# Turning the masks of a graph network by DMA instead of on TensorE, eleven in each of two stages

## The chip, the core and the metric

One of the eight cores of a Trainium2 chip runs the whole program. The metric is device microseconds of one execution. The engines are called as the profile calls them: PE is TensorE (PEld its weight loads), DVE is VectorE, ACT is ScalarE, POOL is GpSimd and SP is SyncE, which only issues DMAs here.

## What is computed

A graph of 2708 nodes has 512 features a node (x, float32) and a dense symmetric adjacency matrix adj (int32, about 2.3% ones, with a full diagonal). Four layers follow each other, each as `x = layernorm(x + layer(x, adj))`. What matters for the change is layer 0:

```
Ab   = adj > 0
keep = Ab & (cumsum(Ab, axis=1) <= 64)        # the first 64 neighbours of a row
cnt  = keep.sum(axis=1)
nb   = (keep @ x) / max(cnt, 1)
x0   = leaky(x @ W_line.T + b_line) + where(cnt > 0, leaky(nb @ W_nb.T + b_nb), 0)
```

Layer 1 uses all neighbours (`mask @ x / deg`) and a pair of dense products; layers 2 and 3 are graph attention over the same mask, layer 3 with a feed-forward net behind it. So every layer reads one mask, and layer 0 reads besides which ones are among the first 64 of their row.

## The kernel before, in words

The rows are cut into 22 tiles of 128 (the last has 20). The mask is needed transposed, since a matmul contracts over partitions. It lies in one tile that stays to the end, `maskT`, 128 partitions x 22 tiles x 2816 columns in fp8: element (p, j, c) belongs to neighbour 128 j + p of node c. Its sign tells two things: -1 is a neighbour among the first 64, +1 a later one, 0 none. Layer 0 takes `Relu(-maskT)` (line 369, into `kT`), later layers take it as it is different from zero (line 525).

A mask, that is the 128 rows of one row tile, is made in these steps:

- `load_mask` (line 272): a DMA on POOL's queue reads 128 x 2708 int32 and casts to bf16, into a buffer `m`.
- `count` (line 277): one activation on ACT over the whole width; its accumulator gives the row's degree, `cnts`.
- `place` (lines 283 and 286): on DVE a scan along the row counts up from -64.5 and stops at 0.5 (`OP.min` with a half), and a product with the mask leaves a negative number on the first 64 ones, a positive one on the rest and 0 elsewhere. In stage 1 a row is done in two parts, in stage 2 in four, each part a scan and a product.
- `turn` (lines 288 to 304): 22 PE transposes of 128 x 128 (line 295) against a bf16 identity, in three groups of up to eight, each group into one PSUM bank; after each group ACT takes the sign from PSUM into `maskT` (line 299). Last, a small DMA on POOL's queue copies the 20 rows of the last row tile to partitions 32 to 51 (line 302).

The program runs in stages. Only the first two are touched.

**Stage 1** (line 307 on) walks the 22 row tiles. Per tile it transposes x on PE (line 133), copies it to SBUF on ACT (line 135, `xT`), multiplies it by W_nb (line 259; the result is split into `yH` on ACT, line 231, and `yL` on DVE, line 236) and by W_line (line 259 again, into the single buffer `pm1`), whose result gets its bias and its leaky relu on DVE (lines 352 and 195) and goes to DRAM through POOL's queue (line 354). The order of PE is written out by hand here: `pe(...)` ties each PE instruction behind the one before. Among these steps the first `HERE` masks are made: one per tile in most tiles, with the turn of a mask a tile after its count. `issue_after` ties the count behind `yH` and the two parts of the scan behind `yL` and behind the relu. Mask buffers `m` are three. x is fetched on SP's queue into three buffers (line 173).

**Stage 2** (line 360 on) is the sum `keep @ x W`. The row tiles are taken in blocks, first the two last (20 and 21), then five blocks of four (`cuts`), and the masks are made in that same order (`turns`). A block runs over the 22 column tiles j: ACT makes `kT` for the next j (line 369, two buffers), and PE adds `kT.T @ yH` and `kT.T @ yL` into one PSUM bank per row tile (line 496). A block needs its masks complete. At each j two generators are advanced by a step: `todo`, which finishes the row tiles of the block before (lines 414 to 421, DVE mainly, with `r0` and x fetched on SP's queue), and `both`, which runs the remaining masks (`other_masks`), then the weights of layer 1 (`weights1`), then small vectors of layers 2 and 3 (`vectors`). `both` stands behind the `kT` of the next j (`issue_after`). Each `yield` ends a step. A mask of `other_masks` takes eleven steps before the change: one for the count and one empty, four for the parts of the scan, two empty ones, three for the groups of the turn. Its buffers are two rooms, `w` (the place of a weight) and `spare`.

Behind stage 2 follow layer 1 (a second stage of products, in which DVE takes the signs out of `maskT`, then sums over the mask, line 547) and the two attention layers with the feed-forward net. Between the engines the order of instructions is set by a scheduler that keeps the program's dependencies and the `issue_after` ties; each engine then runs its own list in order, and waits on semaphores.

Of the kernel before, what the change touches and what calls it, by code (L numbers as in the profile page):

```python
# [11 lines left out]
BF16 = mybir.dt.bfloat16  # L12
F8 = mybir.dt.float8e4
AF = mybir.ActivationFunctionType
# [4 lines left out]
P = 128  # L19
# [7 lines left out]
STEP = 2.0 ** 68  # L27
# [3 lines left out]
def kernel(  # L31
# [9 lines left out]
    nc = tc.nc  # L41
    N = x.shape[0]
    NT = -(-N // P)
    FULL = N // P
# [5 lines left out]
    def rows(t):  # L50
        return min(P, N - t * P)
# [11 lines left out]
    identb = const.tile([P, P], BF16, name="identb")  # L63
    nc.vector.tensor_copy(identb, ident)
    G = 8
# [16 lines left out]
    maskT = big.tile([P, NT, NT * P], F8, name="maskT")  # L82
# [12 lines left out]
    few = N - (NT - 1) * P  # L95
    LAST, TWIN = NT - 1, 32
# [61 lines left out]
    def early(first, n, make):  # L158

        made = {}  # L160

        def get(i, **how):
            for j in range(len(made), min(i + first + 1, n)):
                made[j] = make(j, **how)
            return made[i]
        return get
# [36 lines left out]
    with ExitStack() as phase:  # L203
        yp = phase.enter_context(tc.tile_pool(name="y", bufs=1))
        cnts = yp.tile([P, NT], F32, name="cnts")
# [56 lines left out]

        HERE = NT - 8
        cuts = [(b, min(b + 4, NT)) for b in range(0, NT, 4)]
        cuts = cuts[-1:] + cuts[:-1]
        turns = [t for b in cuts for t in range(*b)]

        def load_mask(i, m):  # L270
            n = rows(turns[i])
            nc.gpsimd.dma_start(m[:n], adj[turns[i] * P:turns[i] * P + n, :], max_dma_last_dim=N * 2)
            return m

        def count(i, m):
            t, n = turns[i], rows(turns[i])
            nc.scalar.activation(m[:n], m[:n], AF.Sigmoid, bias=gate[:n], scale=STEP, accum_out=cnts[:n, t:t + 1])

        def place(i, m, places, part, of):

# [4 lines left out]
                                         OP.add, OP.min)  # L285
            return nc.vector.tensor_mul(m[:n, c0:c1], m[:n, c0:c1], places[:n, :c1 - c0])

        def turn(i, m, psum, order=as_it_comes):
            t, n = turns[i], rows(turns[i])
            for g0 in range(0, NT, G):  # L290
                g1 = min(g0 + G, NT)
                ps = psum()
                for j in range(g0, g1):
                    w = rows(j)
                    order(nc.tensor.transpose(ps[:w, j - g0, :n], m[:n, j * P:j * P + w], identb[:n, :n]))
                parts = [(P, g0, min(g1, FULL))] + ([(rows(FULL), FULL, NT)] if g1 > FULL else [])
                for w, a, b in parts:
                    if a < b:
                        nc.scalar.activation(maskT[:w, a:b, t * P:t * P + n], ps[:w, a - g0:b - g0, :n], AF.Sign,
                                             saturate=False)  # L300
                if g1 == NT:
                    nc.gpsimd.dma_start(maskT[TWIN:TWIN + few, LAST, t * P:t * P + n],
                                        maskT[:few, LAST, t * P:t * P + n])
                yield

        def rows_of(src):
            return early(2, NT, lambda t: fetched(src, t, rows(t)))

        with ExitStack() as ph:
            st = ph.enter_context(tc.tile_pool(name="l0a", bufs=1))  # L310
            wnT, wlT = weight(), weight2
            room = [maskT[:, G + k, :4 * D].bitcast(F32) for k in range(2 * KD)]

            xs = rows_of(x)
            xTs = early(0, NT, lambda t, order=as_it_comes: transposed(ahead, ps_tr, xs(t), rows(t), "xT", order))

            transpose_weight(room[:KD], ps_tr, wnT, l0_w_nb, (nc.sync, nc.scalar))
            lows = {}  # L320
            for t in range(2):
                xT = xTs(t, order=pe)
                lows[t] = keep_y(t, P, product(xT, P, wnT, 0, pe))
            transpose_weight(room[KD:], ps_tr, wlT, l0_w_line)
            b_line = bias(bcast(l0_b_line, D))
            masks = early(1, HERE, lambda i: load_mask(i, st.tile([P, N], BF16, name="m", bufs=3)))
            masks(0)
            nc.gpsimd.memset(maskT[:, NT - 1, :], 0.0)
            nc.gpsimd.memset(maskT[:, :, N:], 0.0)
            counted = turned = 0  # L330
            for t in range(NT):
                n = rows(t)
                if t > 1:

                    lows[t] = keep_y(t, n, product(xTs(t, order=pe), n, wnT, 0, pe, sums() if t % 2 else None))
                xT = xTs(t)
                if t + 1 < NT:
                    xTs(t + 1, order=pe)
                while turned < counted - (t + 2 < NT):
                    for _ in turn(turned, masks(turned), lambda: sums(BF16, (P, G, P)), pe):  # L340
                        pass
                    turned += 1
                now = counted < min(HERE, -(-(t - 1) * HERE // (NT - 5)))
                if now:
                    m, places = masks(counted), st.tile([P, N // 2], BF16, name="places", bufs=1)
                    with tc.issue_after(highs[t].ins):
                        count(counted, m)
                    with tc.issue_after(lows[t].ins):
                        place(counted, m, places, 0, 2)
                pm = product(xT, n, wlT, 1, pe)  # L350
                u = sm.tile([P, D], F32, name="u")
                nc.vector.tensor_add(u[:n], pm[:n], b_line[:n])  # L352
                low = rows_made = leaky(u[:n], u[:n])
                nc.gpsimd.dma_start(r0_dram[t * P:t * P + n, :], u[:n])
                if now:
                    with tc.issue_after(low.ins):
                        place(counted, m, places, 1, 2)
                    counted += 1
# [3 lines left out]
        with ExitStack() as ph:  # L362
# [9 lines left out]
            def other_masks():  # L372

                def room(i):
                    r = (ahead.tile([P, 2 * KD * (D + 2 * H)], BF16, name="w", tag="w", bufs=1) if i % 2 else
                         st.tile([P, 2 * KD * D], BF16, name="spare", tag="spare"))
                    m = r[:, :N]
                    load_mask(i, m)
                    return m, r[:, N:N + N // 4 + 1]

                got = {HERE: room(HERE)}
                for i in range(HERE, NT):
                    if i + 1 < NT:
                        got[i + 1] = room(i + 1)
                    m, places = got.pop(i)
                    if i == HERE:
                        for _ in range(5):
                            yield
                    count(i, m)
                    yield  # L390
                    yield
                    for part in range(4):
                        place(i, m, places, part, 4)
                        yield
                    yield
                    yield
                    psum = (ps_mm.tile([P, G, P], BF16, name=f"pm{k % 2}") for k in range(3))
                    for _ in turn(i, m, lambda: next(psum)):
                        yield
                nc.vector.tensor_scalar(iso, cnts, 0.5, None, op0=OP.is_lt)  # L400
                nc.vector.tensor_scalar(rdeg, cnts, 1.0, None, op0=OP.max)
                nc.vector.reciprocal(rdeg, rdeg)
# [83 lines left out]
            for i, b in enumerate(cuts):  # L486
                ts_ = range(*b)
                pa = {t: sums() for t in ts_}
                for j in range(NT):
                    if j + 1 < NT:  # L490
                        nxt, nxt_made = kept(b, j + 1)
                    elif i + 1 < len(cuts):
                        nxt, nxt_made = kept(cuts[i + 1], 0)
                    for t in ts_:
                        for y in halves(j):
                            nc.tensor.matmul(pa[t], kT[:, (t - b[0]) * P:(t - b[0] + 1) * P], y[:, j, :],  # L496
                                             start=(j == 0 and y is yH), stop=(j == LAST))
                    kT = nxt
                    if j % 3:
                        next(todo, None)  # L500
                    with tc.issue_after(nxt_made.ins):
                        next(both, None)
                with tc.issue_after(nxt_made.ins):
                    reciprocals(slice(*b))
                us = {}
                for t in ts_:
                    n = rows(t)
                    us[t] = st.tile([P, D], F32, name=f"u{t - b[0]}")
                    nc.scalar.activation(us[t][:n], pa[t][:n], AF.Copy, scale=rkeep[:n, t:t + 1])
                todo = finish(ts_, us)  # L510
# [6 lines left out]
            for t in range(NT):  # L517
                n = rows(t)
# [989 lines left out]
```

## Time and profile before

| what | value |
|---|---|
| time, median of 3 runs | 2926.25 us (2925.69 to 2927.17) |
| the profiled execution: time | 2926.44 us |
| its span, first to last instruction | 2924.5 us |
| mean granted TensorE clock | 0.996 |
| PE / DVE / ACT / POOL busy | 2842.8 / 1983.5 / 1499.8 / 244.8 us |
| first and last PE transpose of a mask, stage 1 | 50.1 and 195.2 us |
| the same, stage 2 | 221.2 and 376.1 us |
| first sum (line 496) | 202.54 us |

A line of the order of time gives start, duration, engine, line, operation, output and inputs, shapes and how many instructions are merged; in brackets stands the idle time of the engine before it, and who ended it. In the table of DMA issues the last number is the median time from issue to landing. In the table of queues stand packets, megabytes and the time of their packets as a share of 16 DMA engines over the span. PE's matmuls are pipelined, so the time of a run of matmuls is read from start to start.

### The profile page before, as it was taken

The numbers are of one execution on the slowest core, as the hardware profiler recorded it, in microseconds if no ns is written. First come the engines' busy times: TensorE is split into PE (matmuls) and PEld (weight loads), VectorE is DVE, ScalarE is ACT, GpSimd is POOL, SyncE is SP. The second block draws the span as 40 slices with busy tenths as digits, with TensorE's granted clock in tenths as the row PEclk, the third lists the DMA queues.
The fourth block names the chain that finished last, engine by engine and source line by source line (L and its number), as shares of the span: only waits on it lengthen the run. The fifth ranks groups of instructions, "written<-read, shape, count | busy, mean of one in ns | idle before, by whom it ended". The sixth has DMA issues, their size and how long they took to land. (4 is left out here: it accounts for less than half of the span.)

```text
span 2924.5 us, 36470 instructions
## 1 busy us (share of the span) xinstructions
PE 2842.8 (97%) x14370; PEld 1584.3 (54%) x14370; DVE 1983.5 (68%) x2341; ACT 1499.8 (51%) x1749; POOL 244.8 (8%) x387
## 2 busy tenths in 40 slices
PE   8999999999999999999999999999999999999997
PEld 4557766458888333444466443444375555555555
DVE  6866637542334999999978999999954435435342
ACT  3546532112322999999965999999951000000001
POOL 1111101101110000000012000000200010100000
PEclk9999999999999999999999999999999999999999
DMA  5633426322222111111143111110161000000000
GB/s 130 131 88 72 109 80 184 123 63 91 83 72 78 33 37 36 35 45 39 38 142 122 37 37 36 45 51 34 35 160 60 4 26 15 26 15 16 15 22 21
DMA packets 122518, 181.58 MB, mean 62 GB/s; under 512 B 43007, under 2 KB 67908, under 8 KB 122338
## 3 DMA queue, kind: packets, MB, share of 16 engines
q1 hardware_dynamic: 92470, 117.50, 13.5%
q0 software_dynamic: 18864, 57.45, 6.9%
q10 hardware_dynamic: 11004, 4.22, 0.6%
q8 instruction: 115, 1.88, 0.3%
q14 instruction: 65, 0.53, 0.1%
HBM read 148.91 MB, written 44.65 MB: 66 GB/s over the span
## 5 line engine op out<-in xcount | busy, mean ns | idle before, releaser
L752 DVE SCALAR_TENSOR_TENSOR e<-v_bc,ucol,maskT 128x1408 f32<-128x1408 f32 (+3 forms) x804 | 1133.7, 1477 | 322.3 <-PE pn L1135 312.8
L781 ACT ACTIVATE c<-e,bcol 128x1300 fp8e4<-128x1300 f32 (+2 forms) x688 | 956.6, 1412 | 63.4 <-DVE e L752 18.6
L953 PE MATMUL po<-e,R 128*64 128x512 f32 (+3 forms) x4224 | 894.7, 548 | 26.3 <-DVE e L752 24.3
L953 PEld LDWEIGHTS po<-e,R 128*64 128x64 f32 (+1 forms) x4224 | 333.4, 136 | 554.7 <-issue 390.4
L1135 PE MATMUL pn<-e,R 128*128 128x512 f32 (+3 forms) x1056 | 403.0, 545 | 1.1 <-DVE lin L1155 0.3
L1135 PEld LDWEIGHTS pn<-e,R 128*128 128x128 f32 (+1 forms) x1056 | 183.9, 190 | 197.1 <-issue 181.5
L1085 ACT ACTIVATE w<-pl,b 128x256 f32<-128x256 f32 (+1 forms) x88 | 40.9, 465 | 371.0 <-PE pl L1083 371.0
L496 PE MATMUL acc<-yH,kT 128*128 128x512 f32 x484 | 195.2, 409 | 4.7 <-ACT kT L369 4.5
L547 PE MATMUL acc<-yH,mf 128*128 128x512 f32 x484 | 185.0, 389 | 0.0
L496 PE MATMUL acc<-yL,kT 128*128 128x512 f32 x462 | 180.8, 391 | 0.0
L547 PE MATMUL acc<-yL,mf 128*128 128x512 f32 x462 | 179.7, 389 | 0.0
L122 POOL TENSOR_TENSOR ln_rs<-ln_rs,half 128x1 f32<-128x1 f32 (+1 forms) x88 | 53.0, 602 | 1397.7 <-DVE ln_rs L121 1348.4
L674 PE MATMUL pm<-w,xT 128*128 128x264 f32 (+1 forms) x704 | 165.1, 387 | 3.4 <-ACT xT L135 1.6
L259 PE MATMUL pm<-weight,xT 128*128 128x512 f32 (+1 forms) x344 | 158.4, 604 | 8.2 <-DVE u L352 6.8
L1083 PE MATMUL pl<-lin 128*128 128x256 f32 (+1 forms) x704 | 155.9, 376 | 3.4 <-DVE lin L982 3.4
L1108 PE MATMUL pl<-lin,w 128*128 128x512 f32 x336 | 150.8, 593 | 0.0
L1083 PEld LDWEIGHTS pl<-lin 128*128 128x128 f32 x704 | 131.2, 193 | 34.5 <-issue 15.8
L674 PEld LDWEIGHTS pm<-w,xT 128*128 128x128 f32 (+1 forms) x704 | 129.7, 190 | 25.8 <-ACT xT L135 3.6
L544 ACT CAST mf<-maskT 128x1024 fp32r<-128x1024 fp8e4 (+1 forms) x66 | 64.5, 978 | 151.7 <-PE acc L547 148.1
L259 PE MATMUL pm<-w,xT 128*128 128x512 f32 x296 | 133.6, 594 | 5.8 <-ACT xT L135 2.1
L369 ACT ACTIVATE kT<-maskT 128x512 fp32r<-128x512 fp8e4 (+1 forms) x132 | 77.5, 594 | 115.6 <-PE acc L496 114.4
L853 PE MATMUL pd<-c,parts_c 128*12 128x384 fp8e4 (+2 forms) x2688 | 128.3, 307 | 0.0
(251 smaller groups left out, 2656.2 us busy)
## 6 DMA issues: line engine op xcount, KB each, us to landing
rows<-x_dram SPq DMA_DIRECT2D x63, 256.0 KB
v_bc<-v_dram SPq DMA_DIRECT2D x16, 704.0 KB
rows<-in_x_dram SPq DMA_DIRECT2D x42, 256.0 KB
x_dram<-u POOLq DMA_DIRECT2D x42, 256.0 KB, 2.5
v_bc<-v_dram SPq DMA_DIRECT2D x16, 650.0 KB
m<-in_adj_dram POOLq DMA_DIRECT2D x13, 677.0 KB, 6.9
r_dram<-u POOLq DMA_DIRECT2D x21, 256.0 KB, 2.3
rows<-r_dram SPq DMA_DIRECT2D x21, 256.0 KB
```

The costliest lines, as they stand in the source:

```text
L259: order(nc.tensor.matmul(pm[:m], xT[:, k, :m], w[:, k, :], start=(k == 0), stop=(k == KD - 1)))
L369: made = nc.scalar.activation(kT[:, :w], maskT[:, j, b[0] * P:b[0] * P + w], AF.Relu, scale=-1.0)
L496: nc.tensor.matmul(pa[t], kT[:, (t - b[0]) * P:(t - b[0] + 1) * P], y[:, j, :], start=(j == 0 and y is yH), stop=(j == LAST))
L547: nc.tensor.matmul(pa, mf[:, j - g0, :], y[:, j, :], start=(j == 0 and y is yH), stop=(j == LAST))
L674: nc.tensor.matmul(pm[a][:m, :D // 2 + heads], xT[:, k, :m], w[:, k, a, :D // 2 + heads], start=(k == 0), stop=(k == KD - 1))
L752: self.made = nc.vector.scalar_tensor_tensor(e[:, :w], v[:, :w], ucol[:, j, h:h + 1], maskT[:, j, c0:c0 + w], op0=OP.max, op1=OP.mult)
L781: nc.scalar.activation(c[:, :w], e[:, :w], AF.Sigmoid, bias=bcol[:, j, h:h + 1], scale=STEP, saturate=False)
L853: pe(nc.tensor.matmul(p[32 * g:32 * g + 12, :c1 - c0], parts_c[:, j, h, :], c[:, c0:c1], start=(i == 0 and h == hs[0]), stop=(i == NT - 1 ...
L953: pe(nc.tensor.matmul(po[i][HO * k:HO * k + HO, :c1 - c0], R2[at, j, h * HO:(h + 1) * HO], e[at, a:a + c1 - c0], start=(i_ == 0), stop=(i_ ...
L1083: nc.tensor.matmul(pl[:, :w], self.lin1[:, k, f * P:(f + 1) * P], h[:, k, :w], start=(k == 0), stop=(k == KD - 1))
L1108: nc.tensor.matmul(pl[:n], gT[:, f, (t - t0) * P:(t - t0) * P + n], self.lin2[:, f, :], start=(f == 0), stop=(f == KF - 1))
L1135: nc.tensor.matmul(pn[k][:, :w], R2[at, j, k * P:(k + 1) * P], e[at, :w], start=(j == 0), stop=(j == NT - 1))
```

## The change

The masks are no longer turned on PE but by one transposing DMA each, on SP's queue: `dma_start_transpose(into, m)` turns 128 x 2816 bf16 into 22 blocks of 128 x 128. It lands in SBUF, in `into`, and ACT takes the signs from there into `maskT`, in four pieces (8, 8, 5 tiles and the last tile of 20 rows).

- `HERE` goes from 14 to 11: eleven masks are made in stage 1 and eleven in stage 2.
- In stage 1 `into` is one of four places in that part of `maskT` itself (columns of tiles 10 to 17) that is not written yet. The signs of a mask are taken when the second mask after it is turned.
- In stage 2 `into` is the tile `weight2`, the weight of stage 1's second product, one place for all. First the signs of the last two masks of stage 1 are taken. A mask then takes eight steps: count and an empty one, four parts, two empty ones, with the transfer issued ahead of those; its signs are taken in the steps of the next mask's parts 2 to 4.
- Buffers `m` are 2816 wide instead of 2708, and the 108 columns behind are cleared on POOL each time.
- At j = 7 and 15 of each block `both` is advanced by two steps instead of one.

In the changed kernel the lines shift: 295 and 299 are gone, the transfer is at line 289, the signs at 294, the small copy at 296, the bias of stage 1 (352) at 355, `kT` (369) at 372, the finishing lines 414 to 421 at 426 to 433, the sums (496) at 508, the copies `u` out of PSUM (509) at 522.

```diff
-        HERE = NT - 8
+        HERE = NT - 11
...
-        def turn(i, m, psum, order=as_it_comes):
+        def turn(i, m, into):
+            nc.sync.dma_start_transpose(into, m)
+
+        def signs(i, into):
             t, n = turns[i], rows(turns[i])
-            for g0 in range(0, NT, G):
...
-                    order(nc.tensor.transpose(ps[:w, j - g0, :n], m[:n, j * P:j * P + w], identb[:n, :n]))
...
-                        nc.scalar.activation(maskT[:w, a:b, t * P:t * P + n], ps[:w, a - g0:b - g0, :n], AF.Sign,
-                                             saturate=False)
...
+            for w, a, b in [(P, a, min(a + G, FULL)) for a in range(0, FULL, G)] + [(few, FULL, NT)]:
+                nc.scalar.activation(maskT[:w, a:b, t * P:t * P + n], into[:w, a:b, :n], AF.Sign, saturate=False)
                 yield
+            nc.gpsimd.dma_start(maskT[TWIN:TWIN + few, LAST, t * P:t * P + n],
+                                maskT[:few, LAST, t * P:t * P + n])
+
+        idle = [maskT[:, :, (HERE - 1 + 2 * i) * P:(HERE + 1 + 2 * i) * P].bitcast(BF16) for i in range(4)]
...
+            def mask_rows(i):
+                m = st.tile([P, NT * P], BF16, name="m", bufs=3)
+                nc.gpsimd.memset(m[:, N:], 0.0)
+                if rows(turns[i]) < P:
+                    nc.gpsimd.memset(m, 0.0)
+                return load_mask(i, m)
...
-                while turned < counted - (t + 2 < NT):
-                    for _ in turn(turned, masks(turned), lambda: sums(BF16, (P, G, P)), pe):
+                while turned < counted:
+                    for _ in signs(turned - 2, idle[(turned - 2) % 4]) if turned > 1 else ():
                         pass
+                    turn(turned, masks(turned), idle[turned % 4])
                     turned += 1
...
-                    m = r[:, :N]
+                    m = r[:, :NT * P]
+                    nc.gpsimd.memset(m[:, N:], 0.0)
                     load_mask(i, m)
...
+                into = weight2.rearrange("p k c -> p (k c)").bitcast(BF16)[:, :NT * P].rearrange("p (t n) -> p t n", n=P)
...
                     if i == HERE:
-                        for _ in range(5):
-                            yield
+                        for k in (HERE - 2, HERE - 1):
+                            yield from signs(k, idle[k % 4])
                     count(i, m)
                     yield
                     yield
                     for part in range(4):
                         place(i, m, places, part, 4)
+                        if part:
+                            next(left, None)
                         yield
+                    for _ in left:
+                        pass
+                    turn(i, m, into)
+                    left = signs(i, into)
                     yield
                     yield
-                    psum = (ps_mm.tile([P, G, P], BF16, name=f"pm{k % 2}") for k in range(3))
-                    for _ in turn(i, m, lambda: next(psum)):
-                        yield
+                for _ in range(4):
+                    yield
+                for _ in left:
+                    yield
...
-                        next(both, None)
+                        for _ in range(1 + (j % 8 == 7)):
+                            next(both, None)
```

More of the change, by code (lines that the diff above doesn't have):

```diff
@@ L271, in load_mask @@
             n = rows(turns[i])
-            nc.gpsimd.dma_start(m[:n], adj[turns[i] * P:turns[i] * P + n, :], max_dma_last_dim=N * 2)
+            nc.gpsimd.dma_start(m[:n, :N], adj[turns[i] * P:turns[i] * P + n, :], max_dma_last_dim=N * 2)
             return m
@@ L276, in count @@
             t, n = turns[i], rows(turns[i])
-            nc.scalar.activation(m[:n], m[:n], AF.Sigmoid, bias=gate[:n], scale=STEP, accum_out=cnts[:n, t:t + 1])
+            nc.scalar.activation(m[:n, :N], m[:n, :N], AF.Sigmoid, bias=gate[:n], scale=STEP, accum_out=cnts[:n, t:t + 1])
         def place(i, m, places, part, of):
@@ L286, in place @@
             return nc.vector.tensor_mul(m[:n, c0:c1], m[:n, c0:c1], places[:n, :c1 - c0])
-        def turn(i, m, psum, order=as_it_comes):
+        def turn(i, m, into):
+            nc.sync.dma_start_transpose(into, m)
+        def signs(i, into):
             t, n = turns[i], rows(turns[i])
-            for g0 in range(0, NT, G):
[L291 to L298, printed above, removed]
-                        nc.scalar.activation(maskT[:w, a:b, t * P:t * P + n], ps[:w, a - g0:b - g0, :n], AF.Sign,
-                                             saturate=False)
-                if g1 == NT:
-                    nc.gpsimd.dma_start(maskT[TWIN:TWIN + few, LAST, t * P:t * P + n],
-                                        maskT[:few, LAST, t * P:t * P + n])
+            for w, a, b in [(P, a, min(a + G, FULL)) for a in range(0, FULL, G)] + [(few, FULL, NT)]:
+                nc.scalar.activation(maskT[:w, a:b, t * P:t * P + n], into[:w, a:b, :n], AF.Sign, saturate=False)
                 yield
+            nc.gpsimd.dma_start(maskT[TWIN:TWIN + few, LAST, t * P:t * P + n],
+                                maskT[:few, LAST, t * P:t * P + n])
+        idle = [maskT[:, :, (HERE - 1 + 2 * i) * P:(HERE + 1 + 2 * i) * P].bitcast(BF16) for i in range(4)]
         def rows_of(src):
@@ L325 @@
             b_line = bias(bcast(l0_b_line, D))
-            masks = early(1, HERE, lambda i: load_mask(i, st.tile([P, N], BF16, name="m", bufs=3)))
+            def mask_rows(i):
[4 more added lines that the diff above has]
+                return load_mask(i, m)
+            masks = early(1, HERE, mask_rows)
             masks(0)
@@ L376, in room @@
                          st.tile([P, 2 * KD * D], BF16, name="spare", tag="spare"))
-                    m = r[:, :N]
+                    m = r[:, :NT * P]
+                    nc.gpsimd.memset(m[:, N:], 0.0)
                     load_mask(i, m)
-                    return m, r[:, N:N + N // 4 + 1]
-                got = {HERE: room(HERE)}
+                    return m, r[:, NT * P:NT * P + N // 4 + 1]
+                got, left = {HERE: room(HERE)}, iter(())
+                into = weight2.rearrange("p k c -> p (k c)").bitcast(BF16)[:, :NT * P].rearrange("p (t n) -> p t n", n=P)
                 for i in range(HERE, NT):
```

## The prediction, made before the changed kernel ran

> **What bounds the kernel now.** I read the busy shares and the 40 slices first, then the order of time on PE (TensorE), ACT (ScalarE) and DVE (VectorE) in the first two stages, then the DMA queues and issues.
>
> ```profile
> PE 2842.8 (97%) x14370; PEld 1584.3 (54%) x14370; DVE 1983.5 (68%) x2341; ACT 1499.8 (51%) x1749; POOL 244.8 (8%) x387
> PE   8999999999999999999999999999999999999997
> PEclk9999999999999999999999999999999999999999
> ```
>
> PE is busy in every slice at the full granted clock: time is won only where PE gets less to do, and lost only where it waits. The change touches stage 1 (products, and masks counted and turned, to 202.54 us where the first L496 starts) and stage 2 (the sums: six blocks of 22 column steps). Stage 1 on PE, then on DVE:
>
> ```profile
> 123.23 0.60 PE L133 MATMUL ps_tr<-ident,rows 128*128 128x128 f32 x4
> 123.66 1.49 PE L295 MATMUL acc<-identb,m 128*128 128x128 bf16 x22
> 125.81 3.70 PE L259 MATMUL pm<-weight,xT 128*128 128x512 f32 x8 [0.66 <-DVE u L352]
> ```
>
> ```profile
> 146.19 2.98 DVE L283 TENSOR_TENSOR_SCAN places<-m,over 128x1354 bf16<-128x1354 bf16 x1 [2.34 <-ACT m L277]
> 149.09 0.67 DVE L352 TENSOR_TENSOR u<-pm,bias 128x512 f32<-128x512 f32 x1
> ...
> 155.53 2.98 DVE L283 TENSOR_TENSOR_SCAN places<-m,over 128x1354 bf16<-128x1354 bf16 x1
> 158.55 0.87 DVE L286 TENSOR_TENSOR m<-m,places 128x1354 bf16<-128x1354 bf16 x1
> 159.33 0.68 DVE L352 TENSOR_TENSOR u<-pm,bias 128x512 f32<-128x512 f32 x1
> ```
>
> A turn holds PE from 71.61 to 73.03 in an unhindered step, 1.42 us. Behind several turns PE also waits for DVE: L352, which empties the one buffer pm1, stands behind a 3 us scan. Stage 2 on ACT, and what a count does there to PE:
>
> ```profile
> 244.28 2.54 ACT L277 ACTIVATE spare<-spare,gate 128x2708 bf16<-128x2708 bf16 x1
> 246.72 0.18 ACT L277 ACTIVATION_READ_ACCUMULATOR spare<-spare,gate 128x1 f32 x1
> 246.81 1.14 ACT L369 ACTIVATE kT<-maskT 128x512 fp32r<-128x512 fp8e4 x2
> 249.69 0.63 ACT L369 ACTIVATE kT<-maskT 128x512 fp32r<-128x512 fp8e4 x1 [1.74 <-PE acc L496]
> ```
>
> ```profile
> 247.48 0.50 PE L496 MATMUL acc<-yH,kT 128*128 128x512 f32 x1 [0.26 <-ACT kT L369]
> ```
>
> Each 1.82 us column step of PE needs one kT from ACT (0.63 us, two buffers, some 1.2 us to spare). Whatever holds ACT longer holds PE. This carries the forecast.
>
> **The new operation.** No row shows a DMA that turns. Let Y be its time from issue to landing, for 128 x 2816 bf16, 704 KB.
>
> ```profile
> q1 hardware_dynamic: 92470, 117.50, 13.5%
> q10 hardware_dynamic: 11004, 4.22, 0.6%
> ...
> spare<-in_adj_dram POOLq DMA_DIRECT2D x4, 677.0 KB, 6.2
> w<-in_adj_dram POOLq DMA_DIRECT2D x4, 677.0 KB, 9.0
> oT_dram<-oT POOLq DMA_DIRECT2D x4, 704.0 KB, 4.1
> ```
>
> Below: the same bytes, merely copied, land 4.1 us after issue (oT). Above: a turn of 128-column blocks moves rows of 256 B, 2816 of them, 176 on each of 16 DMA engines. By q10 a packet (384 B on average) takes 0.6% x 16 x 2924.5 / 11004 = 25 ns, by q1 (1270 B) 68 ns: 4.5 or 12.0 us, and 1.6 us more for the shortest landing among the small copies of L302: 6.1 or 13.6 us. I take 9, about midway between the two (geometric mean 9.1), because the source rows are small as in q10 but the queue is q1; 4.1 and 13.6 are kept for the range. If it were done as 22 separate pieces, each landing as L302's quickest, 35 us.
>
> The Trainium skill speaks against the change: "VectorE: DVE Perf Modes", section "The three transpose paths", gives 1309 ns for a 128x128 bf16 block by the DMA crossbar against 390 ns on TensorE; 22 in a row would be an estimated 28.8 us. "DMA: Bandwidth & Descriptors", section "Latency and other measured facts", gives 261 GB/s for a transposing DMA, an estimated 2.8 us for 704 KB before any latency, with which the change would win. In this trace TensorE's block costs 1.42/22 = 65 ns, pipelined, so the 390 ns overstates what is removed.
>
> **Stage 1: gains 10.5 us.**
> - Removed: 13 turns x 1.42 + 0.79 for the mask of 20 rows = 19.3 us of PE.
> - DVE: 11 masks instead of 14, two in every three steps. Two masks cost it 2 x 9.56 (the step at which it paced PE, 116.25 to 125.81) and three steps of the rest 2 us, 21 us in all; PE's three steps, now without turns, take 3 x 7.3 = 21.9. So it fits on average, but not inside a pair. From the end of the first product (0): scan at 3.85 or 4.7, the second mask's L355 (old L352) ends near 17 by the spacing shown above, and PE wants pm1 at 2 x 7.3 + 0.43 = 15.0. Five pairs x 2 us, and 1.3 for the table load in the first, make 11.4 us of waiting; before it was 3.9 + 5.0 = 8.9. Cost 2.5.
> - A new wait: in ACT's new order the first kT (its room overlies the mask buffers of stage 1) waits until the last transfer of the stage has landed, ahead of the copies yH and xT that PE needs. It is issued some 14 us after its step began, and the copies take 1.9 more; PE wants xT at 18.6. Cost Y - 2.7 = 6.3. Behind the same kT wait on ACT the signs of masks 9 and 10.
> - At no cost: the signs two masks later (16 to 18 us after issue, so hidden up to such a Y); x loads behind transfers on SP's queue (fetched two steps of 7.3 us ahead); memsets of 108 columns on POOL.
>
> **Stage 2: loses 21 us.**
> - Removed: 8 turns. A block of pure sums is 22 x 1.82 = 40.0; blocks with two turns last 43.63 and 44.29, so 1.9 for a turn with what hangs on it: 15.2.
> - Block 0 has two columns: a step is 0.92 us, a kT 0.42. Eight signs (1.0, 1.0, 0.7, 0.25, twice) stand between its kTs, with the first count: 3 us beyond the steps' slack.
> - Eleven counts instead of 8, and those of blocks 1 to 3 right behind the four u copies (2.4 us), where the spare time is gone: 1.3 to 1.5 instead of 0.26. Cost 3.5.
> - Mask 11's signs: its scans end 9.0 us after its count (4 x 2.22), and ACT comes to the sign 9.95 us after the count: wait Y - 0.95 and 0.7 for signs between short steps, 8.7 in all. Behind it stand all kTs.
> - Mask 13's load uses mask 11's room: landing, 0.9 on POOL and 9.0 (w) to land; ACT reaches its count some 3.1 us earlier.
> - Blocks 1 to 3 hold three masks each. ACT takes a mask's first sign ten kTs (18.2 us) after its count. DVE has 3 x 8.9 for scans and 4 x 3.9 for finishing four row tiles, 42.3 in a 40 us block, most finishing in the first half. In blocks 2 and 3 the second mask's scans end 31.0 us after the first count, its sign is due at 31.7 with 1.4 to spare: PE waits Y - 2.1 = 7 in each. Block 1 finishes less: 4. Together 18. The one landing room (weight2) binds later: Y + 5.1 against a 13.3 us mask step, so from Y = 8.2.
> Sum: -15.2 + 3 + 3.5 + 8.7 + 3.1 + 18 = +21.
>
> Later stages read finished masks and are left as they are. Total -10.5 + 21 = +10.6: from the profiled execution's 2926.44 (span 2924.5 and 1.94 around it; the median of the runs is 2926.25, 0.2 less, which I neglect) to **2937**.
>
> **By Y**, same terms: 4.1: stage 1 -15.4, stage 2 +2.2, 2913. At 6.1: -13.4 and +8.7, 2922. At 13.6: -5.9, and the landing room gives (13.6 + 5.1 - 13.3) x 8 = 43 in place of the 18, so +51: 2971. Even near 7.
>
> **Rivals.**
> 1. A quick transfer (Y under 6) wins: place, the signs of stage 2; price, 2913 to 2921, say **2917**. For it: oT's 4.1, and DMA share only 0.29 to 0.41 in the sum blocks. Against: 256 B rows, and mask loads of 6 to 9 us beside it. It decides for faster from Y = 6 down. Chance 0.30.
> 2. Even (Y 6 to 8.2): the turns saved on PE return as waits of ACT: **2926**, 0.19.
> 3. Forecast, Y 8.2 to 13.6: **2937**, 0.38.
> 4. A transfer by pieces (Y 14 to 35): each mask of stage 2 then takes Y + 5.1 instead of 13.3, 11 x 12 = 130 us at Y = 20: **3050** or more, 0.13. For it: nothing in this trace has turned data by DMA; against: 176 packets an engine do not reach it.
> That the change doesn't do what it says is excluded for PE (its new order has no L295), but "two masks later" holds in stage 1 only: in stage 2 the signs come one mask later, and there the loss lies.
>
> **Numbers.** Chances come from the four cases: faster by over 0.2% (5.9 us, about what this measurement can tell from no change) 0.30, within 0.19, slower 0.51. The range runs from the lower bound, 2912, to 2990, past the upper bound of Y; it leaves out case 4 and a little.
>
> **What would show it.** Y: landing of L289. Stage 1: PE waiting for L355 about 2 us behind each second mask, and one wait of some 6 us near the first kT. Stage 2: ACT idle before L294 until the DMA, PE idle before L508 until kT, blocks of 47 us or more. Wrong if Y is under 6 or over 14, if SP is held by issuing, or if mask loads slow down beside the transfers.

## The result and the profile after

The median went from 2925.7 us (five runs, 2920.88 to 2927.17) to 2946.9 us (five runs, 2937.86 to 2947.72): a ratio of 1.0069, with a 95% interval of 1.0052 to 1.0085. The forecast was 2937, slower; the change is slower, by about twice the forecast loss. The parts of the loss are not the forecast ones, as the stages show at once:

| what | before | after | forecast difference | measured |
|---|---|---|---|---|
| stage 1, to the first sum | 202.5 us | 222.9 us | -10.5 | +20.4 |
| stage 2, first sum to the first sum of layer 1 | 441.1 | 447.6 | +21 | +6.5 |
| from there to the end of the span | 2280.9 | 2274.9 | 0 | -6.0 |
| span of the profiled execution | 2924.5 | 2945.4 | +10.6 | +20.9 |

The last row but one is code that the change leaves as it is. Over the profiled executions of this case, one of each kernel, that stretch lies between 2274.6 and 2281.9 us, and no run tells why. So up to some 7 us of a difference between two spans say nothing of the first two stages, and the experiments are read by stage.

The busy shares and the slices of the changed kernel, against those shown of before:

```profile
PE 2831.0 (96%) x13886; PEld 1565.6 (53%) x13886; DVE 1983.5 (67%) x2353; ACT 1501.3 (51%) x1749; POOL 249.9 (8%) x410
PE   7788899999999999999999999999999999999997
PEclk9899999999999999999999999999999999999999
```

PE has 484 instructions less and is busy 11.8 us less, and yet the first five slices show seven and eight tenths, where before only the first was under nine. The loss is idle time in stage 1, and there the granted clock dips as well (0.83 from 100 to 150 us, where before it was 1.00). PE's waits between 44 us and the end of stage 1 (total, times, longest):

```profile
PE acc L259 <- ACT xT L135: 13.0, 3, 8.7
PE pm L259 <- ACT xT L135: 11.4, 3, 4.8
PE pm L259 <- DVE u L355: 6.8, 7, 1.8
```

Before there was no wait for xT there at all, and 6.4 us for the bias line (352, now 355). Two of the new waits in PE's order of time:

```profile
62.00 3.60 PE L259 MATMUL pm<-weight,xT 128*128 128x512 f32 x8
70.39 5.40 PE L259 MATMUL pm<-w,xT 128*128 128x512 f32 x8 [4.79 <-ACT xT L135]
...
93.52 3.60 PE L259 MATMUL pm<-weight,xT 128*128 128x512 f32 x8
105.83 6.53 PE L259 MATMUL acc<-w,xT 128*128 128x512 f32 x8 [8.71 <-ACT xT L135]
```

Eight products take 3.60 us when PE runs on. Behind these waits they take 5.40 and 6.53: a wait is paid twice, once as idle time and once in the clock behind it, since the granted clock is 0.67 over the first of these two groups and 0.55 over the second. Five such groups of stretched products (5.40, 6.53, 6.56, 6.71, 5.40) cost 12.6 us over 3.60 each. What ACT was doing ahead of xT at 69.75:

```profile
57.86 1.88 ACT L294 ACTIVATE maskT<-maskT 128x1024 fp8e4<-128x1024 bf16 x3
68.64 0.74 ACT L294 ACTIVATE maskT<-maskT 128x160 fp8e4<-128x160 bf16 x3 [8.90 <-DMA maskT<-m]
69.28 0.56 ACT L231 CAST yH<-acc 128x512 fp32r<-128x512 f32 x1
69.75 0.58 ACT L135 COPY xT<-ps_tr 128x512 f32<-128x512 f32 x1
```

It stood 8.90 us before a sign, and the transfer it stood for had been issued only at 59.85, on SP's queue:

```profile
59.85 5.43 SPq L289 DMA_TRANSPOSE maskT<-m  x1
```

The mask of the sign at 68.64 is the one of 20 rows (128x160 is 8 x 20 columns), the second mask; the transfer at 59.85 is the second, too. So the signs are not taken two masks later. The text of the program says so, but in ACT's own list the first sign of a mask stands directly behind the issue of its transfer, ahead of yH and xT of the next tile, for all nine masks that are signed in stage 1 (the last two are signed in stage 2). ACT waits 71.7 us there in all:

```profile
ACT maskT L294 <- DMA maskT<-m: 71.7, 9, 12.5
```

The sum of stage 1 nearly closes with that. Before the change there was one stretched group, too, so that 1.8 of the 12.6 us are not new:

```profile
62.50 5.40 PE L259 MATMUL pm<-weight,xT 128*128 128x512 f32 x8 [2.11 <-DVE u L352]
```

-19.3 for the turns (the forecast term), +24.4 for waits for xT, +10.8 for stretched products, +0.4 for line 355, and +2.1 already at 43 us (1.66 of it another stretched group at 22.85 us, 5.36 instead of 3.70) make +18.4 of the measured +20.4; 2.0 us are not put down to any of these.

In stage 2 what was forecast is found. Blocks 0 to 3 end 34.8, 41.5, 49.8 and 47.5 us after their beginnings (before 30.0, 43.6, 44.3, 44.3), and the longer ones hold lines of this kind on ACT and PE:

```profile
333.35 1.13 ACT L372 ACTIVATE kT<-maskT 128x512 fp32r<-128x512 fp8e4 x2
340.56 1.06 ACT L294 ACTIVATE maskT<-weight 128x1024 fp8e4<-128x1024 bf16 x1 [6.07 <-DMA weight<-w]
341.52 0.61 ACT L372 ACTIVATE kT<-maskT 128x512 fp32r<-128x512 fp8e4 x1
```

```profile
342.18 0.79 PE L508 MATMUL acc<-yH,kT 128*128 128x512 f32 x1 [4.22 <-ACT kT L372]
```

ACT comes to a sign before its transfer has landed, the next kT stands behind it, and PE runs dry. In stage 2 PE waits 18.4 us for kT in all, before 4.5.

### The profile page after: what moved, and what is told of

Read it like the earlier page. It is cut to its first block, busy times and chain, and to the rows that moved or that the text cites. A ratio compares the mean times of both kernels' runs of the same rounds, so it can differ in the third digit from the quotient of the medians.

```text
span 2945.4 us, 35603 instructions
## 1 busy us (share of the span) xinstructions
PE 2831.0 (96%) x13886; PEld 1565.6 (53%) x13886; DVE 1983.5 (67%) x2353; ACT 1501.3 (51%) x1749; POOL 249.9 (8%) x410
## 3 DMA queue, kind: packets, MB, share of 16 engines
q10 hardware_dynamic: 11004, 4.22, 0.6%
## 5 line engine op out<-in xcount | busy, mean ns | idle before, releaser
L508 PE MATMUL acc<-yH,kT 128*128 128x512 f32 x484 | 198.7, 416 | 19.8 <-ACT kT L372 18.4
L259 PE MATMUL pm<-w,xT 128*128 128x512 f32 x296 | 140.1, 618 | 14.6 <-ACT xT L135 13.5
```

The lines of the kernel that those rows point to most:

```text
L259: order(nc.tensor.matmul(pm[:m], xT[:, k, :m], w[:, k, :], start=(k == 0), stop=(k == KD - 1)))
```

## The experiments

**Theory A**: stage 1 loses because ACT's list has the signs directly behind their transfers. **Theory B**, the recorded steps: those signs are free, stage 2 loses; if x is late in stage 1, then because the transfer holds SP. In the expectations "first sum" is the end of stage 1. The lines of the kernels shift by a few; the bias line is 355, 356, 358, 373 or 374. The kernel before, beside them on the same chips, took 2927 to 2929 us.

### e1: the signs of stage 1 really two masks later

```
                 while turned < counted:
-                    for _ in signs(turned - 2, idle[(turned - 2) % 4]) if turned > 1 else ():
-                        pass
+                    with tc.issue_after(highs[t].ins):
+                        for _ in signs(turned - 2, idle[(turned - 2) % 4]) if turned > 1 else ():
+                            pass
```

> The changed kernel, with one tie more: in stage 1 the signs of a mask stand on ACT behind the copy yH of the tile in which they are written in the program, two masks after their own transfer. In the changed kernel's trace they stand directly behind the issue of their own transfer, ahead of yH and xT, and PE waits there 24.4 us for xT, with runs of eight products behind five of these waits that take 5.4 to 6.7 us instead of 3.6 (12.6 us more). Theory A (the loss of stage 1 is this order on ACT): the waits for xT fall under 4 us and the slow runs go with them; first sum at 186 to 194 us instead of 222.9; time about 2913 (2906 to 2920). Theory B (the recorded steps: these signs cost nothing, stage 2 is what loses; what delays xT in stage 1 is the transfer itself, which holds SP's queue and so the loads of x): first sum at 215 us or later, time 2938 or more.

Measured: 2911.2 us, 0.9941 of the kernel before (0.9923 to 0.9959). First sum at 183.1 us, 39.8 earlier than in the changed kernel and a little under the 186 to 194 of theory A; stage 2 takes 446.9 us, as there (447.6). ACT's order in stage 1 now, and PE's waits in the same stretch as above:

```profile
68.95 0.59 ACT L135 COPY xT<-ps_tr 128x512 f32<-128x512 f32 x1
69.43 2.82 ACT L294 ACTIVATE maskT<-maskT 128x1024 fp8e4<-128x1024 bf16 x4
72.16 2.54 ACT L277 ACTIVATE m<-m,gate 128x2708 bf16<-128x2708 bf16 x1
```

```profile
PE pm L259 <- DVE u L356: 4.7, 6, 1.8
PE pm L259 <- ACT xT L135: 1.6, 1, 1.6
```

The signs follow xT and wait for nothing, the waits for xT went from 24.4 to 1.6 us, and the stretched products with them. The same number of transfers on the same queue, with SP no shorter at each (3.3 to 8.4 us), no longer matters: theory A, and not B. One tie makes the loser a kernel that beats both.

### e2 and e3: each stage alone

e2 has stage 1 by DMA and stage 2 on PE; e3 the other way round. In both the turns on PE are the old function, under the name `turn_pe`. First e2 (its landing places lie as in e7, below):

```
-        HERE = NT - 11
+        HERE = NT - 8
...
-                    turn(i, m, into)
-                    left = signs(i, into)
                     yield
                     yield
...
+                    psum = (ps_mm.tile([P, G, P], BF16, name=f"pm{k % 2}") for k in range(3))
+                    for _ in turn_pe(i, m, lambda: next(psum)):
+                        yield
```

> Stage 1 by DMA with the signs as the changed kernel has them, but fourteen masks as before; stage 2 turns its eight masks on PE as before (eleven steps a mask, eight signs ahead of the first). Theory A (stage 1 loses by its order on ACT): fourteen masks instead of eleven meet such waits, first sum at 223 us or later, time 2940 to 2960. Theory B (recorded steps: stage 1 gains 10.5 us, stage 2 loses): first sum near 190 to 195 us, time 2913 to 2918.

Measured: 2947.2 us, 1.0059 (1.0039 to 1.0079); first sum at 227.1 us. PE waits there for xT nine times, 29.4 us, and stage 2 takes 440.9 us, as before the change (441.1). With stage 1 alone by DMA (fourteen masks here) the loss is about that of the whole change, as A has it.

And e3:

```
-                while turned < counted:
-                    for _ in signs(turned - 2, idle[(turned - 2) % 4]) if turned > 1 else ():
+                while turned < counted - (t + 2 < NT):
+                    for _ in turn_pe(turned, masks(turned), lambda: sums(BF16, (P, G, P)), pe):
                         pass
-                    turn(turned, masks(turned), idle[turned % 4])
...
-                        for k in (HERE - 2, HERE - 1):
-                            yield from signs(k, idle[k % 4])
+                        for _ in range(5):
+                            yield
```

> Stage 1 turns on PE as before, but eleven masks; stage 2 by DMA as the changed kernel has it (eleven masks of eight steps, one landing room), without the eight signs ahead of the first mask. Theory A: first sum near 198 us (three turns of 1.42 us less than before), stage 2 as in the changed kernel, from first sum to the first sum of layer 1 some 444 to 448 us against 441 before; time 2924 to 2932. Theory B (recorded steps, stage 2 loses 21 us): 455 us or more from first sum to first sum, time 2938 or more.

Measured: 2929.3 us, 1.0004 (0.9994 to 1.0013), as A had it, but by other parts: first sum at 193.1 us (9.4 earlier than before, with three masks less on PE and on DVE; some 4.5 was expected), and stage 2 455.4 us, 14.3 more than before. That is A's miss and B's bound met: without the eight signs ahead every mask comes three steps earlier, ACT's six waits for landings make 22.6 us instead of 18.6, and PE waits 25.2 us for kT instead of 18.4. This points to the place of a mask's steps, and not to the transfer alone, as what sets the loss of stage 2.

### e5: a second landing room in stage 2, the signs three steps later

```
+                into = [weight2..., maskT[:, :, 18 * P:20 * P].bitcast(BF16)]
...
-                        if part:
+                        if part > 1:
                             next(left, None)
                         yield
-                    for _ in left:
-                        pass
-                    turn(i, m, into)
-                    left = signs(i, into)
-                    yield
-                    yield
+                    turn(i, m, into[i % 2 * (i + 1 < NT)])
+                    for _ in range(2):
+                        next(left, None)
+                        yield
+                    left = signs(i, into[i % 2 * (i + 1 < NT)])
```

> As e1_signs_behind_yH, and in stage 2 two landing rooms in turn (weight2, and the columns of tiles 18 and 19 of maskT, which are not written yet) with each sign three steps later in the next mask. Theory A for stage 2 (PE's 18.4 us of waits for kT in the sums come from signs that ACT reaches ahead of their transfer, which takes 5.2 to 6 us): the waits of PE for kT fall under 8 us; 12 to 16 us faster than e1, about 2899. Rival (the waits come from the counts and the shorter steps, and the room and the place of the signs do not matter): within 4 us of e1.

By its edit it also leaves out ten of the eleven small copies (296) of stage 2, so its mask is incomplete and it is no kernel to use. Measured: 2950.4 us, 1.0069 (1.0043 to 1.0094), with the tie of e1: 39 us more than e1, where 12 to 16 less were expected. Stage 2 takes 481.4 us, 34.5 more than in e1, and the first sum, with the same stage 1, comes at 189.5. ACT's waits in stage 2:

```profile
ACT kT L373 <- DMA maskT<-w: 44.4, 5, 12.2
```

kT reads maskT; every second transfer now lands in maskT, in columns that this kT does not read, and yet kT waits for it. So e5 does not test the idea of two rooms: a landing place inside a tile that is being read makes the readers wait for the landing. Whether two rooms outside maskT would help was not tried.

### e6: nine steps a mask

```
                     left = signs(i, into)
                     yield
                     yield
+                    yield
```

> As e1_signs_behind_yH, and in stage 2 a mask takes nine steps instead of eight (one empty step more behind the issue of the transfer, so that ACT comes to the signs one column step, 1.82 us, later). In e1's trace PE waits 18.6 us for kT in the sums, 15 times, the longest 4.0. Theory A (ACT reaches the signs before a transfer of 5.2 to 6 us has landed, by 1 to 6 us in six of the eleven masks): each of these waits is shorter by up to 1.8 us, the waits for kT together 8 to 12 us; time 2901 to 2906, against about 2911. Rival (the waits are the price of counts behind the copies u and of eight signs ahead of the first mask): waits and time as in e1, within 3 us.

Measured: 2916.0 us, 0.9957 (0.994 to 0.9974): no gain over e1, against A. Stage 2 takes 454.3 us, 7.4 more than in e1, which neither theory has: PE waits 17.0 us for kT instead of 18.6, but 4.4 instead of 1.3 us for the copies u, and 2.7 for a bias line of layer 1. ACT's waits for landings of over 1 us are now three, of 2.98, 8.56 and 3.34 us. Ahead of the longest DVE shows this:

```profile
276.77 1.56 DVE L283 TENSOR_TENSOR_SCAN spare<-spare,over 128x677 bf16<-128x677 bf16 x1
...
283.30 0.69 DVE L431 TENSOR_TENSOR rows<-rows 128x512 f32<-128x512 f32 x1 [3.88 <-DMA rows<-in_x_dram]
...
291.33 0.51 DVE L286 TENSOR_TENSOR spare<-spare 128x677 bf16<-128x677 bf16 x1
```

The four parts of this mask take 15.1 us (the same mask in e1: 12.0; without other work between them 8.8), since the finishing of row tiles, with a wait for a load of x among it, stands between them. The transfer is issued at 292.00, after ACT came to the sign at 288.6. One step more doesn't cover that: here it is DVE's lateness that makes the sign early. With ten and eleven steps, below, no such wait is over 2.3 us.

### e7 to e10: how many masks where

e7: fourteen masks in stage 1 and eight by DMA in eleven steps each in stage 2; e8: the same stage 1, the eight masks on PE as before; e9: twelve and ten (ten steps); e10: thirteen and nine (eleven steps). All with the tie of e1. The diff is that of e7; e9 has NT - 10 and two steps more, e10 NT - 9 and three, and e8 has the stage 2 of e2.

```
-        HERE = NT - 11
+        HERE = NT - 8
-        idle = [maskT[:, :, (HERE - 1 + 2 * i) * P:(HERE + 1 + 2 * i) * P]...
+        idle = [maskT[:, :, (HERE - 2 + 2 * i) * P:(HERE + 2 * i) * P]...
...
                     left = signs(i, into)
                     yield
                     yield
+                    yield
+                    yield
+                    yield
```

> As e1_signs_behind_yH, but fourteen masks in stage 1 as before the change (the four landing places one tile further on), and the eight masks of stage 2 by DMA in eleven steps each, so that their signs come three steps later. Theory A: no transfer is waited for in stage 2, 426 to 432 us from the first sum to the first sum of layer 1 (before 441.1, less eight turns of 1.9), and stage 1 pays only the wait of PE for DVE behind three masks more: first sum 186 to 194; time 2889 to 2898. Rival (DVE cannot hold fourteen masks beside a stage 1 without turns, and becomes its bound): first sum at 198 us or later, time 2903 or more.

> As e7_fourteen_dma in stage 1 (fourteen masks by DMA, signs tied behind yH), but stage 2 turns its eight masks on PE as before the change. Theory A: first sum as in e7, stage 2 as before, about 441 us from first sum to first sum; time 2902 to 2910, 12 to 16 us more than e7: the price of eight turns on PE. Rival (eight masks by DMA gain nothing in stage 2, what PE saves is waited for): within 4 us of e7.

> As e1_signs_behind_yH, but twelve masks in stage 1 and ten in stage 2 of ten steps each. Measured so far: eleven masks in stage 1 end it at 183.1 us and leave 446.9 us to the first sum of layer 1; fourteen end it at 204.6 and 217.2, with 429.3 behind it. Theory D (stage 1 has room on the DMA engines and on DVE for eleven or twelve masks, their share is 0.87 to 1.08 there already, and pays 7 us and more for each mask beyond): first sum 184 to 190, stage 2 438 to 443, time 2903 to 2908. Rival (each mask in stage 1 costs the same from the eleventh on, (204.6 to 217.2 - 183.1)/3 = 7 to 11 us, more than stage 2 gains by one fewer, 5.9): first sum 190 or later, time 2912 or more.

> As e9_twelve with thirteen masks in stage 1 and nine in stage 2, of eleven steps. Theory D: first sum 191 to 200, stage 2 431 to 437, time 2908 to 2915. Rival: first sum 198 to 205, time 2914 to 2920.

| kernel | masks in stage 1 | first sum | stage 2 | median | ratio to before (95%) |
|---|---|---|---|---|---|
| e1 | 11 | 183.1 | 446.9 | 2911.2 | 0.9941 (0.9923 to 0.9959) |
| e9 | 12 | 185.1 | 438.6 | 2910.3 | 0.9954 (0.9932 to 0.9976) |
| e10 | 13 | 197.0 | 434.8 | 2908.0 | 0.9928 (0.991 to 0.9946) |
| e7 | 14 | 217.2 | 429.3 | 2913.9 | 0.9953 (0.9936 to 0.997) |
| e8 | 14, stage 2 on PE | 204.6 | 442.8 | 2925.5 | 0.9993 (0.9984 to 1.0003) |

The stage columns come from one profiled execution of each kernel, and stage 1 differs between executions: e7 and e8 have the same stage 1, and so have e1, e5 and e6 (183.1, 189.5 and 183.3). e9's profiled execution was the shortest of its seven (2901.0 us of 2901.0 to 2926.3); e7's was the longest of its four, 2926.4 us, and the others took 2912.1 to 2914.0, about as much less as e8's first sum is earlier.

Stage 2 came as expected in all four: e7 against e8 shows that eight turns by DMA instead of on PE are worth 13.5 us there, near the 15.2 that were removed, if a mask has eleven steps. In stage 1 e7 and e8 missed: 186 to 194 was expected. ACT and PE in e7, and the stretch from 150 to 190 us with the busy time of PE, PEld, DVE, ACT and POOL, the granted clock, the share of the DMA engines and GB/s:

```profile
177.32 2.55 ACT L277 ACTIVATE m<-m,gate 128x2708 bf16<-128x2708 bf16 x1 [14.18 <-DMA m<-in_adj_dram]
```

```profile
179.05 6.32 PE L259 MATMUL pm<-weight,xT 128*128 128x512 f32 x8 [12.01 <-DVE u L356]
```

```profile
150.00:190.00 40.00, 27.99 (x72) 12.84 (x71) 25.85 (x21) 17.26 (x23) 5.04 (x11) 0.83 1.11 139
```

In this stretch of e7 it isn't DVE's work that holds PE (25.85 us of 40) but a stall of transfers, with the 16 DMA engines at a share of 1.11: a mask issued at 155.87 is waited for until 177.32, a transfer holds SP for 12.53 us, and DVE stood 11.53 us before line 356 for a store of r0. But this is one event of one execution. e8 has the same stage 1 without it. PE's waits there and in e7, from 44 us to the first sum, and e8's stretch from 150 to 190 us:

```profile
PE pm L259 <- DVE u L356: 30.9, 11, 12.0
PE pm L259 <- DVE u L374: 19.5, 10, 3.9
150.00:190.00 40.00, 33.65 (x91) 15.35 (x90) 37.05 (x34) 23.96 (x32) 6.68 (x13) 0.99 0.83 165
```

Here DVE is busy 37.05 of 40 us at a DMA share of 0.83, as the rival had it, and the first sum is still at 204.6. PE's waits for the bias line on DVE rise with the masks of stage 1: 4.7, 7.4, 12.4 and 19.5 us at eleven, twelve, thirteen and fourteen (e1, e9, e10, e8). Nor does a high share alone stop PE: in e1, from 100 to 150 us, it is 1.08, and PE is busy 49.23 of 50 us. So the rival is not refuted. Whether DVE's own work or late loads and counts ahead of it set the bound was not separated.

e9 and e10 fell as theory D said by stage (185.1 and 197.0; 438.6 and 434.8), with e9's median 2 us over its range; that is D's numbers, not its cause. e1, e9 and e10 all beat both kernels; their intervals overlap, so which of them is best stays open.

### e11: the signs behind the count, too

```
                     with tc.issue_after(lows[t].ins):
                         place(counted, m, places, 0, 2)
+                if turned > waiting and turned > 2:
+                    with tc.issue_after(highs[t].ins):
+                        for _ in signs(turned - 3, idle[(turned - 3) % 4]):
+                            pass
```

(`waiting` is `turned` ahead of the loop of the turns, which no longer takes signs.)

> As e1_signs_behind_yH, but in stage 1 the signs stand behind the count of the same tile, too, so that DVE's scans are not held up 2.9 us by them. In e1 PE still waits for L356 in stage 1, 3.7 us behind the 45th microsecond. Theory A (the order on ACT decides in stage 1): the waits for L356 fall by 0 to 3 us, those for xT by none; time 2908 to 2912. Rival (signs behind the count come too late for the first kT or for yH of the next tile): first sum 186 or later, time 2914 or more.

Measured: 2915.3 us, 0.9954 (0.9936 to 0.9971); first sum at 191.0 us. Behind the 45th microsecond PE's waits for the bias line rose from 3.7 to 9.8 us, and those for xT from 1.6 to 2.3. By its numbers that is the rival's side, but what rose is a wait for DVE, which the rival did not name. Which instruction delays what here was not followed further.

## Why the prediction was right, and where it was not

- **Sign and size.** Slower was right, 2937 against 2946.9, well inside the range. But that was luck, two errors that partly cancelled: stage 1 was forecast 30.9 us too low, stage 2 14.5 too high. By the prediction's own sign, "Wrong if Y is under 6", its account was wrong.
- **The step that failed**: "At no cost: the signs two masks later (16 to 18 us after issue, so hidden up to such a Y)". That is what the program's text says; in ACT's list the signs stand directly behind the transfers. The cost was 22.1 us of waits for xT (24.4 less 2.3 at the first kT) and 10.8 of stretched products (12.6 less 1.8). e1 makes the sentence true, and stage 1 ends at 183.1 us, 19.4 under before.
- **Y was mis-sized**: 9 us was taken, midway between bounds; issued with no mask load beside it, a transfer is followed by its sign 5.2 to 5.5 us after issue where ACT stood waiting (6.0 for the last one of stage 1). It lies inside the bounds of 4.1 and 13.6, and by the recorded table alone that is the case of rival 1, which was to win. Rival 1 decided by the wrong stage: with Y at 5.2 the kernel loses as long as the signs of stage 1 stand where they do, and wins with e1.
- **Stage 2's working held, given Y.** Its table gives +2.2 at Y = 4.1 and +8.7 at 6.1, so some +6.1 at 5.3 (between the two in a straight line); +6.5 was measured. For mask 11 ACT was to wait Y - 0.95 = 4.35; it waited 4.37. In blocks 2 and 3 the costly wait on ACT (6.07 and 4.51) is before the signs of the mask counted second in the block, as forecast: its scans end 33.2 and 31.6 us after the block's first count, where 31.0 was forecast. PE waits 4.22 and 2.69 there; Y - 2.1 gives 3.1.
- **DVE's pairs in stage 1** were forecast at 11.4 us of waits of PE; 6.8 came, 4.7 in e1. The 8.9 us set against them for before are too many: the wait of 2.11 us at 62.50 lies in both of the windows added up, and without the second count they are 6.8.
- **The first kT** was forecast at Y - 2.7; its transfer took 6.0, so 3.3; PE waited 2.26 and lost 1.8 more in the products behind.
- **What was left out**: no term of the sum had the clock that dips behind a wait of PE. The Trainium skill has it: "TensorE: Matmul & The Clock Gate", section "Part 1: The HAM clock gate (the "warmup" mystery)", has the clock halve after an idle window of about 3.4 us and recover after as long a busy one. The trace agrees in kind: 1.8 to 3.1 us were lost behind each of the five waits, and the granted clock is at half for 3.4 us or a multiple of it. But an idle time shorter than that page's window was enough: the wait of 2.26 us was followed by 5.40 us instead of 3.60.
- **The estimate weighed against the change**, 22 blocks at 1309 ns one after another, an estimated 28.8 us by "VectorE: DVE Perf Modes", "The three transpose paths", does not hold for one transfer of 22 blocks: 5.2 us, 236 ns a block. The measurement decides. The estimate of 2.8 us by the 261 GB/s of "DMA: Bandwidth & Descriptors", "Latency and other measured facts", was for the bytes alone, ahead of any latency; 720,896 bytes in 5.2 us from issue to sign are 139 GB/s with the latency in it, and no run parts the two.

## What to carry to other kernels

Where a change says "later", look for the place in the engine's own list, with its wait, and name what stands behind it; a scheduler can move an instruction ahead of where the program has it, and one tie that holds it back was worth 39.8 us here. Moving work from a full engine to the DMA queues takes it off the path only if nothing in order waits for the landing, and only while the engines that feed the transfers keep up: here PE's waits for DVE in stage 1 rose from 4.7 us at eleven masks to 19.5 at fourteen. A forecast that is a sum of stages is checked by stage, or two errors pass for one right answer.

## What the runs showed of the hardware

- A transposing DMA of 128 x 2816 bf16, SBUF to SBUF, lands 5.2 to 5.5 us after issue when no mask load runs beside it (6.0 once), and holds SP's queue for 3.3 to 4.0 us of that; in four of these the DMA engines' share was 0.74 to 0.86. Beside a mask load, in stage 1, it took 7.2 to 12.2 us (share 1.11 and 1.12 in two of them), and in e7 single transfers held SP for up to 12.5 us.
- Eight products behind a wait of PE: 5.4 to 6.7 us instead of 3.6 behind all five waits of over 2 us in the changed kernel's stage 1, but in e7 5.40 behind one of 1.91 us and 3.70 behind one of 2.67. In the changed kernel's trace the stretches at half the granted clock start whole multiples of 3.413 us apart (22.80, 70.58, 101.30, 135.44, 166.16 and 210.53 us). With time cut into windows of that length from such a start, in e7 the wait of 1.91 us lies in one window, and that of 2.67 is cut into 1.21 and 1.46. So the place of a wait in these windows may decide. In the twelve traces, of PE's waits of over 1.2 us between 44 us and the first sum, all with 1.91 us or more in one window have a half clock at or behind them, and none with 1.90 us or less. That was seen afterwards, and no run tests it.
- kT waits for a transfer that lands in other columns of the tile it reads (44.4 us in e5). Whether the chip needs that or only the program's dependencies ask for it, the runs do not tell.
